# Cross attention's output and its sums regrouped through a scratch in DRAM instead of by TensorE transposes, with the queries in another order

## The chip, the core and the metric

The kernel runs on one core of a Trainium2 chip, in one launch. The core has five engines that take their instructions in order and work at the same time: TensorE (PE; its weight loads are listed apart as PEld), VectorE (DVE), ScalarE (ACT), GpSimd (POOL) and SyncE (SP), which here does nothing but issue DMAs. Matrix products land in PSUM, and this kernel cuts PSUM into eight banks. The metric is device time in microseconds (us), median of several runs. The kernel before takes 1217.6 us (three runs, 1217.3 to 1218.85).

## The reference

One layer of a perceiver in float32, for 4 sequences of 256 rows of 256 numbers, each with its own context of 4096 rows. Three parts are added to x one after the other: cross attention, a causal linear attention, and a gated feed-forward network. The change concerns the first.

```python
# B = 4 sequences, T = 256 queries, S = 4096 keys, D = 256, 16 heads of 16
Q = layernorm(x) @ Wq.T + bq
K = ctx @ Wk.T + bk
V = ctx @ Wv.T + bv
Q, K, V = (z.reshape(B, -1, 16, 16).transpose(0, 2, 1, 3) for z in (Q, K, V))
dot = einsum('bhsd,bhtd->bhst', Q, K) / sqrt(16)
out = einsum('bhst,bhtd->bhsd', softmax(dot), V)
out = out.reshape(B, T, D)          # the heads are not moved back
x = x + out @ Wh.T + bh
x = x + causal_linear_attention(layernorm(x))
x = x + feed_forward(layernorm(x))
```

The reshape at the end is what the change turns on. `out` has head, query and dimension as its axes, and it is read as 256 rows of 256 without a transpose. So row h*16 + s//16 of the matrix that Wh multiplies holds the 16 queries s = 16*(s//16) .. +15 of one head h, 16 dimensions each: query s stands in the 16 columns from 16*(s%16) on. The product with Wh sums over these columns, so TensorE needs them on partitions: a partition is a pair of s%16 and dimension, and eight values of s%16 make one half (one of the two k chunks) of 128 partitions.

## The kernel before

**Units and windows.** Cross attention is cut into 16 units u = 4b + q, one for each sequence b and group q of four heads. A unit goes through its 4096 keys in 16 windows of 256, so the main loop (L977) makes 256 windows n and one more. A head has 32 partitions: 16 dimensions, and beside them ones that yield the sum of the weights.

**One window.** In order of TensorE: the scores of the window, transposed (pt, L769, 16 matmuls of 256 columns), with the maxima products of a later unit between them (pm, L732, 8 matmuls of 512 columns); then half an item of a key or value product of a later pair of units (pk or pv, both issued by the helper `product4` at L159, 16 matmuls of 256 or 32 of 128 columns); then the product of the weights of the window before with its values (pav, L789, 16 matmuls). VectorE takes four maxima off pm (mx, L739) and adds pav to the unit's running sum (av: L797 in a unit's first window, L799 after). ScalarE makes the exponentials (e, L774) and takes pk and pv out of PSUM (ku, L675; v, L703). Every one of pt, pm, pk, pv, pav takes one of the eight PSUM banks in turn, and so waits for whoever reads the one that held it before. There are key and value items in the windows below n = 232, after which the start of the causal attention fills in; the maxima run out at n = 238.

**What a unit leaves.** av has 128 partitions, 32 for each of four heads, and 256 columns, the queries. In a head's 32 rows, rows 0 to 15 are the weighted sums by dimension and row 16 the sum of the weights, the denominator. A unit's last av is added in window 0 of the next unit, and there `finish(u - 1)` (L801, called at L1010) gives up to three pieces, which `later` (L1012) puts into windows 2, 8 and 10 of the running unit:

- `normalise` (L809): two TensorE transposes of av into pt_x (L815), so that queries are on partitions; a reciprocal of the eight denominators of each partition (rd, L819), a product (on, L821), the value bias added on POOL (L826), and eight DMAs from SP's queue (L830) that gather 16-number runs of on into the rows of xo, of which two units (q even, q odd) share one tile.
- `turn` (L835), for odd q only: two transposes of xo into px (L839) and VectorE's copy to oT (L840).
- `project` (L843), for odd q only: oT times Wh (py1, L847), added to the residual xr on VectorE (L848).

**The end.** Unit 15 has no unit after it. Its three pieces are returned (L1016) and placed by hand: `normalise()` at L541, before the first two loads of the feed-forward weights (`weight_load`, the w_i tiles, on SP's queue through L400) and the first steps of the causal attention; `turn15` and `project15` in the lists `fills[2]` and `fills[3]` (L549, L550). Each w_i is changed to float by ScalarE (`weight`, L405), and the list of fills has one of them in each of the steps 1 to 6. A step of the causal attention has products pa, masks on VectorE (at, L444) and products po (L453), and the feed-forward work follows in later steps.

**The queries.** `queries(b)` (L852) makes one sequence's queries. Its `turn` (L860) transposes the normalised rows by the helper `transposed` (L161): two TensorE transposes into a bank "tr" and one ScalarE copy (L167) to zT, for each half of 128 queries; `project` (L866) multiplies zT by Wq. The column of zT is the query number, and this order is kept by qT, the scores, e and av.

**Bias and other constants.** `load_rest` (L79) is called once, when the first unit's maxima are done (L970). It issues eleven loads on SP's queue, the first of which lays the value bias bv on all 128 partitions (bv_sb, L83). The context's tiles (L651, four buffers) and the rows of keys (L678) are issued by SP too.

**Order.** In both stretches of `manual_schedule` (L539, L883) the order of PE, ACT, DVE and SP is that of the program; POOL is not among them, and its place is set by the scheduler from what its instructions wait for. POOL's own DMA queue holds only the 16 small loads of bk_sb (L74) at the start.

Of the kernel before, what the change touches and what calls it, by code (L numbers as in the profile page):

```python
# [39 lines left out]
def perceiver_layer(  # L40
# [141 lines left out]
    lnp = ctx.enter_context(tc.tile_pool(name="lnp", bufs=2))  # L182
    psum = ctx.enter_context(tc.tile_pool(name="psum", bufs=8, space=PSUM))
# [107 lines left out]
    def start_causal():  # L291
# [78 lines left out]
        tc, xr, load_x, load_rest, ctxT, wq_sb, bq_sb, wkP, bk_sb, wvP, eps, ident, layernorm, transposed, product4,  # L370
        qT, kts, lnp, bank, rest, start_causal)
# [167 lines left out]
    with tc.manual_schedule(engines={ET.PE, ET.Activation, ET.DVE, ET.SP}):  # L539
        normalise, turn15, project15 = finish  # L540
        normalise()  # L541
# [7 lines left out]
        fills[2] += [turn15]  # L549
# [47 lines left out]
def cross_attention(tc, xr, load_x, load_rest, ctxT, wq_sb, bq_sb, wkP, bk_sb, wvP, eps,  # L597
                    ident, layernorm, transposed, product4, qT, kts, lnp, bank, rest, start_causal):
# [21 lines left out]
    with ExitStack() as st:  # L620
# [180 lines left out]
        def finish(u):  # L801

            b, q = divmod(u, NQ)
            av = avs.pop(u)

            def normalise():  # L809
                if q % 2 == 0:  # L810
                    rows_of[b] = lnp.tile([P, D], F32, tag="xo", name="xo")
                xo = rows_of[b]
                pt = bank([P, 2, 4, 32], "pt_x")
                for i in range(2):
                    nc.tensor.transpose(  # L815
                        pt[:, i].rearrange("p j r -> p (j r)"), av[:, i * P : (i + 1) * P], ident
                    )
                rd = lnp.tile([P, 2, 4], F32, tag="rd", name="rd")
                nc.vector.reciprocal(rd, pt[:, :, :, HD])  # L819
                on = lnp.tile([P, 2, 4, HD], F32, tag="on", name="on")  # L820
                nc.vector.tensor_tensor(  # L821
                    on, pt[:, :, :, :HD], rd.unsqueeze(3).to_broadcast([P, 2, 4, HD]), ALU.mult
                )
                bias = rest[0][:, 4 * q * (HD + 1) : 4 * (q + 1) * (HD + 1)].rearrange("p (h e) -> p h e", e=HD + 1)
                for i in range(2):
                    nc.gpsimd.tensor_tensor(on[:, i], on[:, i], bias[:, :, :HD], ALU.add)  # L826
                for i in range(2):
                    for j in range(4):
                        r0 = 64 * (q % 2) + 16 * j + 8 * i
                        nc.sync.dma_start(  # L830
                            out=xo[r0 : r0 + 8, :].rearrange("a (r d) -> a r d", d=HD),
                            in_=on[:, i, j, :],
                        )

            def turn():  # L835
                oT = lnp.tile([P, KC, P], F32, tag="oT1", name="oT1")
                px = bank([P, KC, P], "px")
                for k in range(KC):
                    nc.tensor.transpose(px[:, k, :], rows_of[b][:, k * P : (k + 1) * P], ident)  # L839
                nc.vector.tensor_copy(oT, px)  # L840
                rows_of[b] = oT

            def project():  # L843
                t, oT = 2 * b + q // 2, rows_of.pop(b)
                py = bank([P, D], "py1")
                for k in range(KC):
                    product4(py, oT[:, k, :], rest[1][:, k, :], start=k == 0, stop=k == KC - 1)  # L847
# [35 lines left out]
        with tc.manual_schedule(engines={ET.PE, ET.Activation, ET.DVE, ET.SP}):  # L883
# [93 lines left out]
            for n in range(NU * NS + 1):  # L977
# [113 lines left out]
```

## Time and profile before

| | us |
|---|---|
| runs of the kernel before | 1217.3, 1217.6, 1218.85 |
| the profiled execution | 1217.58 |
| its span, first to last instruction | 1215.9 |

So 1.7 us of the profiled execution lie outside its span. It stands within 0.1 us of the median of the runs, and sums made against it hold for the median.

The stages, with the time in which each engine was busy (TensorE's clock was granted in full, 0.99 to 1.00, in all of them):

| stage | us | PE | DVE | ACT | POOL | DMA share |
|---|---|---|---|---|---|---|
| first keys, queries, first maxima | 0 to 68 | 58.4 | 52.9 | 25.8 | 13.6 | 0.54 |
| loop: constants still loading | 68 to 152 | 82.4 | 64.6 | 50.5 | 6.1 | 0.37 |
| loop with key or value items | 152 to 900 | 747.3 | 575.5 | 456.7 | 6.9 | 0.30 |
| loop, through the start of the causal attention | 900 to 1018 | 118.0 | 97.0 | 67.6 | 9.1 | 0.14 |
| last unit without maxima | 1018 to 1068 | 47.5 | 32.6 | 36.4 | 10.8 | 0.02 |
| causal attention and feed-forward | 1068 to 1216 | 133.6 | 89.1 | 49.8 | 26.2 | 0.08 |

How to read the lines that follow. A group of instructions is named by its engine, its line in the program, its operation and the tiles that it writes and reads ("out<-in", each with partitions x elements). The number before a bar is how many there are; after it stand the total busy time and the mean in ns, and then the engine's idle time just before these instructions with what ended it. In a timeline each line is a run of equal instructions: start, length, engine and line, the count, and in brackets idle time just before it with the instruction that ended it. "SPq" and "POOLq" are DMAs issued from that engine's queue. In a table of stretches, after the stretch and its length, come the busy times of PE, PEld, DVE, ACT and POOL, then the granted clock, the share of the 16 DMA engines and the GB/s moved.

### The profile page before, as it was taken

The page shows a single profiled execution, that of the slowest core. Times are in us where ns is not written, and L with a number is a line of the kernel's source. Part 1 is how long each engine was busy: PE and PEld are TensorE (multiplying, and loading weights), DVE is VectorE, ACT ScalarE, POOL GpSimd, SP SyncE. Part 2 cuts the span into 40 slices and gives each one's busy share as a digit, 9 for nine tenths or more (in the row PEclk, how much of TensorE's full clock was granted, in tenths as well). Part 3 has the DMA queues.
Part 4 walks back from the last instruction along what each step waited for, and adds up shares of the span by engine and source line. Part 5 has one row for each costly group of instructions (what it writes and reads, how often), then busy time and mean ns, then how long its engine had stood idle before and what let it go on. Part 6 is the DMA issues. An engine that isn't in the chain of part 4 may idle for free.

```text
span 1215.9 us, 42635 instructions
## 1 busy us (share of the span) xinstructions
PE 1187.2 (98%) x18000; PEld 801.0 (66%) x18000; DVE 911.6 (75%) x1767; ACT 686.8 (56%) x1429; POOL 72.7 (6%) x147
## 2 busy tenths in 40 slices
PE   7999999999999999999999999999999999979998
PEld 3566667666766677667766776677667755546777
DVE  6887777777777777777777777777788887577653
ACT  3456666666566655665566655666566646853421
POOL 4010000000000000000000000000000102131210
PEclk9999999999999999999999999999999999999999
DMA  6452332233223421332223322322233000020000
GB/s 210 132 197 65 105 107 64 69 101 117 71 63 103 108 86 57 94 102 89 74 84 102 99 74 80 91 97 74 78 99 108 22 2 4 2 69 14 10 10 18
DMA packets 58190, 95.82 MB, mean 79 GB/s; under 512 B 29072, under 2 KB 31760, under 8 KB 58000
## 3 DMA queue, kind: packets, MB, share of 16 engines
q1 hardware_dynamic: 57072, 92.44, 25.3%
q8 instruction: 142, 2.33, 0.8%
q10 hardware_dynamic: 416, 0.66, 0.2%
q14 instruction: 48, 0.39, 0.1%
q0 software_dynamic: 512, 0.00, 0.0%
HBM read 74.17 MB, written 1.05 MB: 62 GB/s over the span
## 4 chain that ended last, share of the span: by engine, by line
PE 93%; DVE 5%; ACT 1%; DMA 1%; issue 0%; DVEq 0%; ACTq 0%
PE pt L769 22%; PE pm L732 18%; PE pav L789 18%; PE pv L159 11%; PE pk L159 11%; PE pd L530 2%; PE pg L518 2%; PE pu L518 1%; PE pq L870 1%; PE pqk L159 1%; PE pa L427 1%; PE py L492 1%; DVE kt L287 1%; DVE mx L739 1%; PE py L159 1%; PE po L453 1%
## 5 line engine op out<-in xcount | busy, mean ns | idle before, releaser
L774 ACT ACTIVATE e<-pt 128x512 f32<-128x512 f32 x1024 | 529.2, 602 | 381.2 <-PE pm L732 357.6
L739 DVE TENSOR_REDUCE mx<-pm 128x1 f32<-128x512 f32 x1024 | 635.6, 684 | 144.8 <-PE pm L732 144.8
L769 PE MATMUL pt<-qa,kt 32*128 32x256 f32 x4096 | 500.0, 388 | 1.3 <-DVE av L799 0.7
L732 PE MATMUL pm<-kt,qT 32*128 32x512 f32 x2048 | 494.6, 616 | 0.0
L769 PEld LDWEIGHTS pt<-qa,kt 32*128 32x128 f32 x4096 | 316.7, 184 | 117.8 <-ACT v L703 43.2
L789 PE MATMUL pav<-e,v 128*32 128x256 f32 x4096 | 269.6, 379 | 0.0
L732 PEld LDWEIGHTS pm<-kt,qT 32*128 32x128 f32 x2048 | 172.0, 184 | 15.6 <-issue 3.7
L789 PEld LDWEIGHTS pav<-e,v 128*32 128x32 f32 x4096 | 129.6, 110 | 72.5 <-issue 3.9
L799 DVE TENSOR_TENSOR av<-pav,av 128x256 f32<-128x256 f32 x240 | 101.8, 424 | 65.3 <-PE pav L789 65.1
L159 PE MATMUL pv<-wv_sb,ctx 128*32 128x128 f32 x4096 | 137.5, 276 | 0.0
L159 PE MATMUL pk<-ctx,wk_sb 128*32 128x256 f32 x2048 | 136.7, 388 | 0.0
L159 PEld LDWEIGHTS pv<-wv_sb,ctx 128*32 128x32 f32 x4096 | 104.2, 109 | 43.5 <-DVE mx L739 42.7
L159 PEld LDWEIGHTS pk<-ctx,wk_sb 128*32 128x32 f32 x2048 | 54.8, 110 | 67.1 <-DVE mx L739 39.0
L675 ACT ACTIVATE ku<-pk,bk_sb 128x256 f32<-128x256 f32 x128 | 63.2, 495 | 10.9 <-PE pk L159 9.6
L826 POOL TENSOR_TENSOR on<-on,bv_sb 128x64 f32<-128x64 f32 x32 | 9.2, 307 | 819.1 <-DVE on L821 819.1
L703 ACT COPY v<-pv 128x256 f32<-128x256 f32 x128 | 51.5, 402 | 9.9 <-PE pv L159 9.9
L288 ACT ACTIVATE kt<-kt,shift 128x512 f32<-128x512 f32 x32 | 22.4, 725 | 12.5 <-DVE kt L287 12.5
L444 DVE TENSOR_TENSOR at<-pa,mask 128x384 f32<-128x384 f32 x32 | 16.3, 551 | 14.2 <-PE pa L432 14.1
L287 DVE TENSOR_SCALAR kt<-pf,low,top 128x512 f32<-128x512 f32 x32 | 23.7, 804 | 2.8 <-PE pf L281 2.6
L518 PE MATMUL pg<-zT,wg 128*128 128x256 f32 x96 | 23.3, 386 | 0.7 <-ACT zT L510 0.7
L518 PE MATMUL pu<-zT,wu 128*128 128x256 f32 x96 | 22.7, 379 | 0.0
L530 PE MATMUL pd<-wd,hT 128*128 128x256 f32 x96 | 21.6, 381 | 0.0
(128 smaller groups left out, 563.4 us busy)
## 6 DMA issues: line engine op xcount, KB each, us to landing
ctx<-in_ctxT_dram SPq DMA_DIRECT2D x128, 512.0 KB
kt<-ku SPq DMA_DIRECT2D x508, 32.0 KB
xo<-on SPq DMA_DIRECT2D x128, 8.0 KB
xr<-in_x_dram SPq DMA_DIRECT2D x4, 256.0 KB
out_dram<-o SPq DMA_DIRECT2D x8, 128.0 KB
wqkv_sb<-in_wqkv_dram SPq DMA_DIRECT2D x1, 768.0 KB
w_i<-in_w_gate_dram SPq DMA_DIRECT2D x2, 384.0 KB
w_i<-in_w_up_dram SPq DMA_DIRECT2D x2, 384.0 KB
```

The source lines that it names most:

```text
L159: nc.tensor.matmul(out[js], lhsT=lhsT[:, js], rhs=rhs, **flags)
L287: nc.vector.tensor_scalar(f, pf.rearrange("p s t -> p (s t)"), low, top, ALU.max, ALU.min)
L518: nc.tensor.matmul(ps[:, i, :], lhsT=w[:, k, ns], rhs=zT[:, k, :], start=k == 0, stop=k == KC - 1)
L530: nc.tensor.matmul(pd, lhsT=hT[:, n, i * P : (i + 1) * P], rhs=wd[:, n, :], start=n == 0, stop=n == NH - 1)
L675: nc.scalar.activation(ku[:, cs], made.pop(), AF.Identity, bias=bk_sb[:, m : m + 1])
L703: nc.scalar.copy(to.rearrange("p t (h d) -> p t h d", d=HD + 1)[:, :, :, :HD], made.pop().rearrange("p t (h d) -> p t h d", d=HD),)
L732: nc.tensor.matmul(pm, lhsT=qT[rows, q, t0 : t0 + P], rhs=kt[rows, c * CH : (c + 1) * CH], start=True, stop=True,)
L739: nc.vector.tensor_reduce(mx[:, i, j, c : c + 1], pm, AX.X, ALU.max)
L769: nc.tensor.matmul(pt[:, i, :], lhsT=kt[rows, ks], rhs=qa[rows, :], start=True, stop=True)
L774: nc.scalar.activation(e, pt, AF.Exp, scale=0.25)
L789: nc.tensor.matmul(pav[32 * h : 32 * h + 32, :], lhsT=v[:, t % KT, c0 : c0 + 32], rhs=es[n, h][:, i, :], start=i == 0, stop=i == 1,)
L799: nc.vector.tensor_tensor(avs[u], pav, avs[u], ALU.add)
```

## The change

The transposes of a unit's result go. What they did (put queries on partitions, regroup into rows, put columns back on partitions) is done by DMAs through a scratch tile in DRAM, and av never passes TensorE again.

- **Queries in another order.** The ScalarE copy out of the bank "tr" now permutes: query s goes to column 16*(s%16) + s//16 of zT, where it went to column s. qT, the scores, e and av keep this order, so that the 16 columns of av with one remainder s%16, which belong to 16 different rows of the matrix that Wh multiplies, lie side by side. `transposed` is folded into `turn`, which has the same two transposes and one copy for each half as before; the copy's output is now strided.
- **Out to DRAM.** `finish(u)` at once issues four DMAs, one for each head, that write 17 rows of av (16 dimensions and the denominators) with their 256 columns to scr, in runs of 16 numbers (64 bytes).
- **Back.** For each half k, one DMA reads the sums into oT, whose partitions are the pairs of s%16 and dimension, and whose columns are 64 of the 128 rows (4 heads by 16 values of s//16) that two units share; and one reads the denominators into dn, each repeated over the 16 partitions that need it.
- **Queue.** These four writes and four reads a unit are issued by POOL for units 0 to 13 and by SP for units 14 and 15. The eight xo DMAs of a unit on SP are gone.
- **Divide.** `divide` is a reciprocal of dn in place (128 partitions x 128 numbers), a product into oT on VectorE, and the bias on POOL: two adds of 64 numbers a partition as before, now with a bias that depends on partition (dimension) and head. `project` is as before but reads this oT. The pieces `normalise` and `turn` are gone, and the two that are left go to windows 4 and 8.
- **Bias.** bvT replaces bv_sb: [128 partitions, 16 heads], made by eight DMAs on SP of 16 rows of 16 single numbers.
- **End.** Unit 15's DMAs are issued where `finish(15)` is called, in the loop's last pass; its divide is in `fills[2]`, where `turn15` was, and its project stays in `fills[3]`. The line `normalise()` goes.

```diff
+    bvT = const.tile([P, H], F32, tag="bvT", name="bvT")
+
     def load_rest():
 
         q = nc.sync
+        for r in range(P // HD):
+            q.dma_start(
+                out=bvT[r * HD : (r + 1) * HD, :],
+                in_=bvP[: H * (HD + 1)].rearrange("(h e) -> e h", e=HD + 1)[:HD],
+            )
         return (
-            load(bvP.partition_broadcast(P), [P, VW], "bv_sb", queue=q),
+            bvT,
             load(whT, [P, KC, D], "wh_sb", queue=q),
...
-    def transposed(dst, src):
-
-        n = src.shape[1] // P
-        ps = bank([P, n, P], "tr")
-        for k in range(n):
-            nc.tensor.transpose(ps[:, k, :], src[:, k * P : (k + 1) * P], ident)
-        nc.scalar.copy(dst, ps)
...
+    dram = ctx.enter_context(tc.tile_pool(name="dram", bufs=2, space=bass.MemoryType.DRAM))
...
-        normalise, turn15, project15 = finish
-        normalise()
+        divide15, project15 = finish
         for n in range(2):
             weight_load(n)
...
-        fills[2] += [turn15]
+        fills[2] += [divide15]
         fills[3] += [project15, norm3]
...
             b, q = divmod(u, NQ)
             av = avs.pop(u)
-
-            def normalise():
-                if q % 2 == 0:
-                    rows_of[b] = lnp.tile([P, D], F32, tag="xo", name="xo")
-                xo = rows_of[b]
-                pt = bank([P, 2, 4, 32], "pt_x")
-                for i in range(2):
-                    nc.tensor.transpose(
-                        pt[:, i].rearrange("p j r -> p (j r)"), av[:, i * P : (i + 1) * P], ident
-                    )
-                rd = lnp.tile([P, 2, 4], F32, tag="rd", name="rd")
-                nc.vector.reciprocal(rd, pt[:, :, :, HD])
-                on = lnp.tile([P, 2, 4, HD], F32, tag="on", name="on")
-                nc.vector.tensor_tensor(
-                    on, pt[:, :, :, :HD], rd.unsqueeze(3).to_broadcast([P, 2, 4, HD]), ALU.mult
+            queue = nc.sync if u >= NU - 2 else nc.gpsimd
+
+            scr = dram.tile([KC, T // 16 // KC, HD + 1, 4, 16], F32, tag="scr", name="scr")
+            for j in range(4):
+                queue.dma_start(
+                    out=scr[:, :, :, j].rearrange("k r e a -> e (k r) a"), in_=av[32 * j : 32 * j + HD + 1, :]
                 )
-                bias = rest[0][:, 4 * q * (HD + 1) : 4 * (q + 1) * (HD + 1)].rearrange("p (h e) -> p h e", e=HD + 1)
-                for i in range(2):
-                    nc.gpsimd.tensor_tensor(on[:, i], on[:, i], bias[:, :, :HD], ALU.add)
-                for i in range(2):
-                    for j in range(4):
-                        r0 = 64 * (q % 2) + 16 * j + 8 * i
-                        nc.sync.dma_start(
-                            out=xo[r0 : r0 + 8, :].rearrange("a (r d) -> a r d", d=HD),
-                            in_=on[:, i, j, :],
-                        )
-
-            def turn():
-                oT = lnp.tile([P, KC, P], F32, tag="oT1", name="oT1")
-                px = bank([P, KC, P], "px")
+            if q % 2 == 0:
+                rows_of[b] = lnp.tile([P, KC, 2, 4, 16], F32, tag="oT1", name="oT1")
+            oT = rows_of[b]
+            dn = lnp.tile([P, KC, 4, 16], F32, tag="dn", name="dn")
+            for k in range(KC):
+                queue.dma_start(out=oT[:, k, q % 2], in_=scr[k, :, :HD].rearrange("r e j a -> r e (j a)"))
+                queue.dma_start(
+                    out=dn[:, k],
+                    in_=scr[k, :, HD].rearrange("r j a -> r (j a)").unsqueeze(1).to_broadcast([P // HD, HD, 64]),
+                )
+
+            def divide():
+                nc.vector.reciprocal(dn, dn)
+                to = oT[:, :, q % 2]
+                nc.vector.tensor_tensor(to, to, dn, ALU.mult)
                 for k in range(KC):
-                    nc.tensor.transpose(px[:, k, :], rows_of[b][:, k * P : (k + 1) * P], ident)
-                nc.vector.tensor_copy(oT, px)
-                rows_of[b] = oT
+                    bias = rest[0][:, 4 * q : 4 * q + 4].unsqueeze(2).to_broadcast([P, 4, 16])
+                    nc.gpsimd.tensor_tensor(to[:, k], to[:, k], bias, ALU.add)
...
-            return [normalise] + ([turn, project] if q % 2 == 1 else [])
+            return [divide] + ([project] if q % 2 == 1 else [])
...
             def turn():
+
                 zT = lnp.tile([P, KC, T], F32, tag="zT1", name="zT1")
                 got.append(zT)
                 for i in range(2):
-                    transposed(zT[:, :, i * P : (i + 1) * P], z[:, i, :])
+                    ps = bank([P, KC, P], "tr")
+                    for k in range(KC):
+                        nc.tensor.transpose(ps[:, k, :], z[:, i, k * P : (k + 1) * P], ident)
+                    nc.scalar.copy(
+                        zT.rearrange("p k (r a) -> p k a r", a=16)[:, :, 8 * i : 8 * i + 8],
+                        ps.rearrange("p k (a r) -> p k a r", r=16),
+                    )
...
-                        for at, piece in zip((2, 8, 10), left):
+                        for at, piece in zip((4, 8), left):
                             later[n + at] = piece
```

More of the change, by code (lines that the diff above doesn't have):

```diff
@@ L369, in perceiver_layer @@
     finish = cross_attention(
-        tc, xr, load_x, load_rest, ctxT, wq_sb, bq_sb, wkP, bk_sb, wvP, eps, ident, layernorm, transposed, product4,
-        qT, kts, lnp, bank, rest, start_causal)
+        tc, xr, load_x, load_rest, ctxT, wq_sb, bq_sb, wkP, bk_sb, wvP, eps, ident, layernorm, product4,
+        qT, kts, lnp, dram, bank, rest, start_causal)
     wout_sb = rest[8]
@@ L597, in cross_attention @@
 def cross_attention(tc, xr, load_x, load_rest, ctxT, wq_sb, bq_sb, wkP, bk_sb, wvP, eps,
-                    ident, layernorm, transposed, product4, qT, kts, lnp, bank, rest, start_causal):
+                    ident, layernorm, product4, qT, kts, lnp, dram, bank, rest,
+                    start_causal):
     nc = tc.nc
@@ L838, in turn @@
                 for k in range(KC):
-                    nc.tensor.transpose(px[:, k, :], rows_of[b][:, k * P : (k + 1) * P], ident)
-                nc.vector.tensor_copy(oT, px)
-                rows_of[b] = oT
+                    bias = rest[0][:, 4 * q : 4 * q + 4].unsqueeze(2).to_broadcast([P, 4, 16])
+                    nc.gpsimd.tensor_tensor(to[:, k], to[:, k], bias, ALU.add)
             def project():
-                t, oT = 2 * b + q // 2, rows_of.pop(b)
+                t = 2 * b + q // 2
@@ L845, in project @@
+                del rows_of[b]
                 py = bank([P, D], "py1")
                 for k in range(KC):
-                    product4(py, oT[:, k, :], rest[1][:, k, :], start=k == 0, stop=k == KC - 1)
+                    product4(
+                        py, oT[:, k].rearrange("p q j a -> p (q j a)"), rest[1][:, k, :], start=k == 0, stop=k == KC - 1
+                    )
                 nc.vector.tensor_tensor(xr[:, t, :], py, xr[:, t, :], ALU.add)
-            return [normalise] + ([turn, project] if q % 2 == 1 else [])
+            return [divide] + ([project] if q % 2 == 1 else [])
@@ L863, in turn @@
                 for i in range(2):
-                    transposed(zT[:, :, i * P : (i + 1) * P], z[:, i, :])
+                    ps = bank([P, KC, P], "tr")
[4 more added lines that the diff above has]
+                        ps.rearrange("p k (a r) -> p k a r", r=16),
+                    )
             def project(q):
```

## The prediction

> **What bounds the kernel now.** I read the page's busy shares and its chain first, then the timeline of two attention windows, the groups by form, the waits and the end. A "window" below is one pass of the main loop (256 keys of one head group).
>
> ```profile
> PE 1187.2 (98%) x18000; PEld 801.0 (66%) x18000; DVE 911.6 (75%) x1767; ACT 686.8 (56%) x1429; POOL 72.7 (6%) x147
> PE 93%; DVE 5%; ACT 1%; DMA 1%; issue 0%; DVEq 0%; ACTq 0%
> ```
>
> TensorE is busy 98% and is 93% of the chain, so every TensorE instruction removed shortens the run, unless TensorE is then made to wait. Whether it waits is read in a window:
>
> ```profile
> 142.59 0.42 DVE L797 COPY av<-pav 128x256 f32<-128x256 f32 x1 [0.28 <-PE pav L789]
> 143.62 2.48 DVE L739 TENSOR_REDUCE mx<-pm 128x1 f32<-128x512 f32 x4 [0.61 <-PE pm L732]
> 144.38 0.59 PEld L159 LDWEIGHTS pk<-ctx,wk_sb 128*32 128x32 f32 x16 [0.33 <-DVE mx L739]
> 144.39 1.07 PE L159 MATMUL pk<-ctx,wk_sb 128*32 128x256 f32 x16
> 146.25 0.44 PE L815 MATMUL pt_x<-ident,av 128*128 128x128 f32 x2
> 146.39 0.42 DVE L799 TENSOR_TENSOR av<-pav,av 128x256 f32<-128x256 f32 x1 [0.28 <-PE pav L789]
> 146.73 0.20 DVE L819 RECIPROCAL rd<-pt_x 128x8 f32<-128x8 f32 x1
> 146.97 0.29 DVE L821 TENSOR_TENSOR on<-pt_x,rd 128x128 f32<-128x128 f32 x1
> ```
>
> The reader is to see that VectorE has a single hole of 0.61 us, between av and the first maximum (mx), and that the next product (pk, elsewhere pv) starts 0.08 us after that first maximum ends (143.62 + 0.68 = 144.30): it takes the PSUM bank that this maximum frees. So 75% busy is not slack: whatever VectorE does beyond the hole delays TensorE one for one, and no later wait gives it back.
>
> **What is removed.** From one av to the next is 3.80 us in a plain window. In the windows that hold the two pt_x transposes it is 4.17 for two units and 4.27 for the twelve after; with the two px transposes it is 4.17. So units 0 to 13 give 2 x 0.37 + 12 x 0.47 = 6.3 us, and seven px pairs give 7 x 0.37 = 2.6: **-8.9 us**. The 4.27 is itself the mechanism above: there "on" starts 0.26 us after rd, a PSUM bank comes free late, and 0.10 us is lost.
>
> **What is added on VectorE.** The divide now works with dimensions on partitions: a reciprocal of 128 numbers a partition where it was 8, then a 128-wide product. The trace has no such reciprocal; three rows bound it:
>
> ```profile
> L819 DVE RECIPROCAL rd<-pt_x 128x8 f32<-128x8 f32 x16 | 3.3, 205 | 0.5 <-PE pt_x L815 0.5
> L471 DVE RECIPROCAL den<-den 128x16 f32<-128x16 f32 x8 | 2.0, 253 | 0.3
> L112 DVE RECIPROCAL ln_rs<-ln_rs 128x2 f32<-128x2 f32 x4 | 0.6, 160 | 4.1 <-ACT ln_rs L109 4.1
> ```
>
> From 2 to 16 elements, both in SBUF, it grows by 93 ns, 6.64 ns an element: 160 + 126 x 6.64 = 1.00 us. The flattest pair (8 to 16) gives 0.93. The Trainium skill ("VectorE: DVE Perf Modes", section "First, the fixed hardware budget") says that reciprocal is an iterated divide with a repeat count of 8; with that page's 0.96 GHz it is 8.33 ns an element, 1.21 us. I take the rows' 1.00. In order after av: 0.34 to the reciprocal's start (146.39 to 146.73), 1.00, a gap of 0.26 (the product waits for two landings and the reciprocal, like the twelve late "on"), and 0.23 until the next instruction starts (0.29, overlapped by 0.06 as the four maxima are). The first maximum comes 1.83 us after av instead of 1.03: 0.80 late, 0.05 of it covered. The program places the divide in windows with pk or pv for 14 units: 14 x 0.75 = **+10.5 us** (5 with 0.93 and a gap of 0.04; 13.5 by the rule). The loop alone nets +1.6.
>
> The bias adds go to POOL, as before (307 ns each, 6% busy). ScalarE's eight zT copies (0.37 each) write with a stride; one pair stands on the path, at 8.62 us: between 0 and +0.7, taken as 0. The load of bvT is eight issues of 16-row, single-element runs in place of one of 0.42: 3 to 5 us more on SP at 69 us, with 1.6 idle there and then four buffers of context ahead (77.77 to 95.97 is waiting): 0.
>
> **The trip through DRAM, units 0 to 13.** POOL issues four writes, waits for them, then issues four reads. The divide stands four windows later, 4 x 3.80 = 15.2 us of cover. The only rows of POOL's queue are the bk_sb loads: 0.48 us an issue, 2.7/5.1/6.7 us (min/median/max) to landing in a stretch where the DMA engines are 93% busy. With 2.7: 0.1 + 4 x 0.48 + 2.2 + 3.0 of data (next paragraph) + 4 x 0.48 + 2.2 = 11.4 us, hidden; with 5.1 it is 16.2, with 6.7 19.4. A write has 272 runs where bk_sb has 16; SP's issue hardly grows with runs (kt, 16 runs: 0.59; xo, 128 runs: 0.61), so I keep 0.48, and the loop's DMA share is 0.2 to 0.4, so I take **hidden, 0**. If it is late, each microsecond costs 14, because DVE waits in order with the maxima behind it.
>
> **How many engines a write uses.** Packets:
>
> ```profile
> 1070.00:1072.00 2.00, 2.00 (x28) 1.53 (x30) 2.00 (x4) 1.17 (x2) 0.34 (x1) 1.00 0.14 13
> DMA packets 58190, 95.82 MB, mean 79 GB/s; under 512 B 29072, under 2 KB 31760, under 8 KB 58000
> ```
>
> In the first row (a window with only xo's 64-byte runs) a share of 0.14 of 16 engines over 2 us moves 26 kB, 406 packets: 11 ns each. A write here (17 rows x 16 runs of 64 bytes) spread like xo costs nothing. But the Trainium skill ("DMA: Bandwidth & Descriptors", section "Why a DMA increments its semaphore by 16 and not by 1") says that a DMA uses the largest number of engines up to 16 that divides the slowest dimension of both sides; 17 leaves one, on SP's queue the same one each time. The page agrees where it can: 29072 small packets, less 16384 of xo, 128 of bq_sb, 512 single words and 11024 completions of the other 689 DMAs, leave 1024 for xo's 128 DMAs, eight each, as 128 and 8 rows give. By spreading a unit's four writes take 0.7 us of data, by the rule 4 x 272 x 11 = 12.0 on SP's queue (3.0 on POOL's, if each write takes another engine). I take the rule, at 11 ns; a write to DRAM may cost more than the SBUF row: 20 ns would add 10.
>
> **Units 14 and 15 are on SP.** Chain: 0.6 + 12.0 + 1.7 (w_i's latency, 2.7 less its data) + 4 x 0.61 + 2.1 = 18.8 us. Unit 14's av ends at 1018.0 and the divide is due behind the av of 1034.6: 2.2 late. VectorE is the busy one there, and its own work grows by 1.0: **+3.2**. The end:
>
> ```profile
> 1066.47 0.42 DVE L799 TENSOR_TENSOR av<-pav,av 128x256 f32<-128x256 f32 x1 [1.79 <-PE pav L789]
> 1068.54 5.28 SPq L830 DMA_DIRECT2D xo<-on  x8
> 1073.93 0.85 SPq L400 DMA_DIRECT2D w_i<-in_w_gate_dram  x2
> 1077.10 0.84 ACT L405 ACTIVATE wg<-w_i 128x768 f32<-128x768 int32 x1 [2.36 <-DMA w_i<-in_w_gate_dram]
> 1082.67 0.41 DVE L840 COPY oT<-px 128x256 f32<-128x256 f32 x1
> 1083.01 1.01 DVE L444 TENSOR_TENSOR at<-pa,mask 128x384 f32<-128x384 f32 x2
> ```
>
> Gone are TensorE's 0.9 (pt_x and its wait) and ScalarE's 2.36: in the built program the first w_i load now stands before the scratch writes. So VectorE reaches the divide at 1079.5. The data lands at 1067.0 + 18.8 = 1085.8; with 1.00 + 0.26 + 0.29 the masks (L444) start at 1087.3, not 1083.0: **+4.3**. Behind the divide stand the masks, on which TensorE's po waits; POOL's bias stands before its own masks. With the writes spread it is -2.5.
>
> **Sum**, against the profiled execution (1217.58, span 1215.9; the median of the runs is 1217.6): -8.9 + 10.5 + 3.2 + 4.3 = +9.1, **1226.7 us**.
>
> **Rivals.** (1) The 17-row writes spread over the engines. Then units 14 and 15 are hidden: -8.9 + 10.5 + 0.6 - 2.5 = -0.3, **1217.3**, not slower; with the cheap end of the divide 1212. For it: 11 ns packets and idle engines. Against: the count above. It decides when a unit's four writes take under about 6 us. (2) POOL's trip is late: 18 us instead of under 15.2 gives 14 x 2.8 = 39, **1266**; at 16.2 it is 1241. For it: the median landing of 5.1 and the unseen issue price; against: that stretch's 93% DMA load. It decides above 15.2.
>
> **How the numbers follow.** Forecast 0.45 (1219 to 1241: divide 5 to 13.5, packets 11 to 20 ns), rival 1 0.28, rival 2 0.27. Within 0.2% (2.4 us, about what a measurement of this kernel can tell from no change): 0.15, mostly rival 1. Faster 0.16, slower 0.69. The range 1213 to 1260 leaves out rival 1's cheapest divides and rival 2 beyond about 2.5 us late.
>
> **What would show it.** Windows with a divide near 4.55 us from av to av and the reciprocal near 1.00 us; no DVE idle time before it on a DMA in units 0 to 13, but some in 14 and 15; scratch writes at 1 completion each; no ScalarE wait for w_i. A reciprocal under 0.5 us, or the DVE waiting in every unit, would make the prediction wrong.

## The result and the profile after

The changed kernel takes **1424.8 us** (four runs, 1424.2 to 1427.5), the kernel before 1217.5 beside it: a ratio of **1.170** (95% interval 1.169 to 1.172). Forecast was 1226.7, with a range to 1260. The profiled execution is 1424.22 us, its span 1422.5.

The busy shares, the chain and two groups of the page, in the order of the page:

```profile
PE 1208.4 (85%) x17952; PEld 810.8 (57%) x17952; DVE 922.5 (65%) x1759; ACT 690.0 (49%) x1429; POOL 212.1 (15%) x259
...
PEclk9999898998989898989899998989898989998999
...
PE 63%; DMA 15%; POOL 7%; DVE 6%; issue 6%; ACT 1%; SPq 1%; POOLq 0%; DVEq 0%; ACTq 0%
...
L815 POOL DMA_DIRECT2D scr<-av x56 | 107.6, 1926 | 688.8 <-DVE av L800 625.5
...
L830 DVE RECIPROCAL dn<-dn 128x128 f32<-128x128 f32 x16 | 15.2, 953 | 180.4 <-DMA dn<-scr 180.4
```

TensorE has 48 instructions fewer and is still busy for 21 us more, because once in every unit its clock is granted only in part (the row PEclk, in tenths; it had nines alone before). A fifth of the chain is now DMA and POOL. VectorE sits idle for 180.4 us before the reciprocal, until the denominators (dn) land. The new reciprocal itself takes 953 ns, near the 1.00 us that was forecast.

One unit in the timeline. Unit 0's last sum ends at 140.03; its divide stands four windows later:

```profile
139.60 0.43 DVE L800 TENSOR_TENSOR av<-pav,av 128x256 f32<-128x256 f32 x1 [0.28 <-PE pav L790]
140.32 5.80 POOL L815 DMA_DIRECT2D scr<-av  x3 [55.36 <-DVE av L800]
...
150.11 1.92 POOL L815 DMA_DIRECT2D scr<-av  x1 [3.99 <-issue]
...
154.79 0.42 DVE L800 TENSOR_TENSOR av<-pav,av 128x256 f32<-128x256 f32 x1 [0.28 <-PE pav L790]
...
164.32 0.61 POOL L823 DMA_DIRECT2D oT<-scr  x1 [12.29 <-DMA scr<-av]
...
169.24 0.95 DVE L830 RECIPROCAL dn<-dn 128x128 f32<-128x128 f32 x1 [14.03 <-DMA dn<-scr]
...
171.18 1.93 PE L167 MATMUL pk<-ctx,wk_sb 128*32 128x256 f32 x16 [14.52 <-DVE mx L740]
172.88 1.93 PE L790 MATMUL pav<-e,v 128*32 128x256 f32 x16
...
176.69 1.07 PE L167 MATMUL pk<-ctx,wk_sb 128*32 128x256 f32 x16
```

From the end of av (140.03) to the reciprocal (169.24) are 29.2 us, of which 15.2 were covered. An issue of a write takes POOL 1.92 us; the fourth is held up by 3.99 more, for which the trace names no cause; the last write lands 12.29 after the end of its issue; the four reads and their landing take 4.9. VectorE, which could have divided at 155.2, waits 14.03 us with the four maxima behind it, and TensorE's pk, which needs the bank that the first maximum frees, waits 14.52. And then pk and pav, 16 matmuls each, take 1.93 us, where pk takes 1.07 a window later. The granted clock (the column before the DMA share, after the busy times of PE, PEld, DVE, ACT and POOL) says why:

```profile
158.00:169.00 11.00, 0.00 (x0) 0.00 (x0) 0.00 (x0) 0.03 (x1) 2.38 (x4) 0.64 0.55 138
169.00:171.00 2.00, 0.00 (x0) 0.00 (x0) 1.73 (x3) 0.00 (x0) 0.40 (x2) 0.50 0.00 0
171.00:173.00 2.00, 1.82 (x20) 0.91 (x24) 1.92 (x4) 0.00 (x0) 0.14 (x1) 0.50 0.00 0
...
175.00:177.00 2.00, 2.00 (x32) 1.43 (x32) 1.38 (x3) 0.65 (x2) 0.00 (x0) 1.00 0.27 61
```

While TensorE idles its clock falls to one half, and it comes back to full only after 3.6 us of work at half rate.

The account of the 206.6 us between the two spans: units 1 to 14, each with the divide of the unit before it, are longer by 11.5 to 17.1 us, 200.5 together. In their fourteen gaps TensorE is idle for 180.3 us; the half-rate work behind them sums to 56.4 us, of which half, 28.2, is lost; the removed transposes give back 8.9. That makes 199.6 of the 200.5. The rest of the 206.6 is 0.8 before the first sum and 5.4 from unit 15 to the end.

### The profile page after: what moved, and what is told of

Read it like the earlier page. It is cut to its first block, busy times and chain, and to the rows that moved or that the text cites. A ratio compares the mean times of both kernels' runs of the same rounds, so it can differ in the third digit from the quotient of the medians.

```text
span 1422.5 us, 42525 instructions
## 1 busy us (share of the span) xinstructions
PE 1208.4 (85%) x17952; PEld 810.8 (57%) x17952; DVE 922.5 (65%) x1759; ACT 690.0 (49%) x1429; POOL 212.1 (15%) x259
## 4 chain that ended last, share of the span: by engine, by line
PE 63%; DMA 15%; POOL 7%; DVE 6%; issue 6%; ACT 1%; SPq 1%; POOLq 0%; DVEq 0%; ACTq 0%
PE pt L770 14%; PE pav L790 13%; DMA scr<-av 12%; PE pm L733 11%; PE pv L167 8%; PE pk L167 8%; POOL scr L815 6%; DMA dn<-scr 3%; PE pd L531 1%; PE pg L519 1%; DVE mx L740 1%; PE pu L519 1%; PE pq L874 1%; POOL oT L823 1%; DVE dn L830 1%
## 5 line engine op out<-in xcount | busy, mean ns | idle before, releaser
L770 PEld LDWEIGHTS pt<-qa,kt 32*128 32x128 f32 x4096 | 320.6, 186 | 128.6 <-ACT v L704 43.2
L790 PE MATMUL pav<-e,v 128*32 128x256 f32 x4096 | 281.1, 392 | 0.3 <-DVE av L800 0.3
L167 PE MATMUL pk<-ctx,wk_sb 128*32 128x256 f32 x2048 | 142.4, 401 | 103.7 <-DVE mx L740 103.7
L815 POOL DMA_DIRECT2D scr<-av x56 | 107.6, 1926 | 688.8 <-DVE av L800 625.5
L167 PE MATMUL pv<-wv_sb,ctx 128*32 128x128 f32 x4096 | 143.5, 284 | 76.6 <-DVE mx L740 76.6
L167 PEld LDWEIGHTS pv<-wv_sb,ctx 128*32 128x32 f32 x4096 | 108.2, 113 | 121.5 <-DVE mx L740 120.0
L830 DVE RECIPROCAL dn<-dn 128x128 f32<-128x128 f32 x16 | 15.2, 953 | 180.4 <-DMA dn<-scr 180.4
L823 POOL DMA_DIRECT2D oT<-scr x28 | 16.8, 601 | 148.6 <-DMA scr<-av 148.6
L288 DVE TENSOR_SCALAR kt<-pf,low,top 128x512 f32<-128x512 f32 x32 | 23.7, 804 | 2.3 <-PE pf L282 2.3
```

The source lines that it names most:

```text
L167: nc.tensor.matmul(out[js], lhsT=lhsT[:, js], rhs=rhs, **flags)
L770: nc.tensor.matmul(pt[:, i, :], lhsT=kt[rows, ks], rhs=qa[rows, :], start=True, stop=True)
L790: nc.tensor.matmul(pav[32 * h : 32 * h + 32, :], lhsT=v[:, t % KT, c0 : c0 + 32], rhs=es[n, h][:, i, :], start=i == 0, stop=i == 1,)
L815: queue.dma_start(out=scr[:, :, :, j].rearrange("k r e a -> e (k r) a"), in_=av[32 * j : 32 * j + HD + 1, :])
L823: queue.dma_start(out=oT[:, k, q % 2], in_=scr[k, :, :HD].rearrange("r e j a -> r e (j a)"))
```

## The experiments

**First question: is it only that the trip is late?** The two first runs move the divide and the project to later windows and leave all else.

```diff
-                        for at, piece in zip((4, 8), left):
+                        for at, piece in zip((10, 12), left):   # late10
+                        for at, piece in zip((6, 10), left):    # late6
```

> Divide and project stand 10 and 12 windows after a unit's last sum instead of 4 and 8; everything else as changed. Theory A (the trip through POOL's queue is simply too long: 29.0 us in the trace against a cover of 4 x 3.80 = 15.2): with 38 us of cover all fourteen stalls go, and with them the half-rate stretch of TensorE behind each. What is left is +0.8 for the strided query copies, -8.9 for the transposes, 14 x about 0.48 = +6.7 for a divide with the measured 0.95 us reciprocal and its 0.04 us gap, and about +5.4 for units 14 and 15: 1217.6 + 4.0 = 1221.6, in 1218 to 1226. Theory B (the scratch traffic hurts beside the wait, by keeping the DMA engines 86% busy while keys and context tiles want them): more than 1240, with TensorE waiting outside the windows that hold a divide.

Measured: **1225.1 us**, ratio 1.0065 (1.0048 to 1.0081). So the lateness of the divide is nearly all of it: 199.7 of the 207.3 us are gone with 38 us of cover. Unit 0's divide now starts without a wait:

```profile
178.20 0.94 DVE L830 RECIPROCAL dn<-dn 128x128 f32<-128x128 f32 x1
```

The writes are as slow as before (1.92 us an issue, median landing 12.0) and the DMA engines as busy (shares of 0.86 to 0.96 in each stretch of 4 us from 144 to 160). SP feels it: its eight issues of key rows beside them take 12.5 us, where they take 5.4 behind sp16's writes. But TensorE loses little by it in the loop. Two places are longer for no reason of the divide's or the project's. One is a window of unit 4, by 1.1 us; what it waits for the trace doesn't say. The other is the passage from unit 13 to unit 14, by some 1.3 us: an instruction of VectorE there (z, L328) takes 1.40 us beside POOL's issue of a write, where it takes 0.41 elsewhere. The same z takes as long in the changed kernel and in late6, and in no run with cheaper issues. So the traffic does cost something beside the wait, but 2 us and not the 20 of theory B. Of the 7.6 us by which its span is longer than that of the kernel before, 7.1 stand after the last sum, where unit 15 still goes out through SP in 17 rows.

> Divide and project stand 6 and 10 windows after a unit's last sum; everything else as changed. VectorE waited 12.5 us a unit at 4 windows, so at 6 it should wait 12.5 - 7.6 = 4.9 us. Theory A1 (each late microsecond costs one, and TensorE's half clock after a long idle time costs 1.9 more a unit only if the idle time is long): the clock stays full after a 5 us stall: 1221.6 + 14 x 4.9 = 1290. Theory A2 (every stall is followed by the half-rate stretch): 14 x 1.9 = 27 more, 1317.

Measured: **1331.5 us**, ratio 1.093 (1.091 to 1.095). VectorE waits 83.0 us for dn in the fourteen units, 5.9 each, where 4.9 was expected; A2's 1317 with 14 x 1.0 more is 1331. TensorE has thirteen gaps of 4.8 to 10.4 us here, and every one is followed by 2.9 to 4.7 us of work at half rate (47.3 together, so 23.7 lost where 27 was expected). One gap of 5.3 us, from 236.83 to 242.13, and the work behind it, with the granted clock as above:

```profile
239.20:242.10 2.90, 0.00 (x0) 0.00 (x0) 1.87 (x4) 0.00 (x0) 0.54 (x2) 0.51 0.05 11
242.10:246.00 3.90, 3.87 (x52) 2.46 (x56) 1.93 (x4) 0.37 (x1) 0.00 (x1) 0.50 0.17 29
```

So a stall of 5 us pays nearly the same clock as one of 14. A2 holds.

**Second question: the queue, or the shape of the write?** sp17 gives all units to SP; sp16 does too, and writes 16 rows a head, with the four denominators in a write of their own.

```diff
-            queue = nc.sync if u >= NU - 2 else nc.gpsimd
+            queue = nc.sync
...
-                    out=scr[:, :, :, j].rearrange("k r e a -> e (k r) a"), in_=av[32 * j : 32 * j + HD + 1, :]
+                    out=scr[:, :, :HD, j].rearrange("k r e a -> e (k r) a"), in_=av[32 * j : 32 * j + HD, :]
                 )
+            queue.dma_start(
+                out=scr[:, :, HD].rearrange("k r j a -> j (k r) a"),
+                in_=av.rearrange("(j r) s -> j r s", r=32)[:, HD],
+            )
```

> All sixteen units' scratch DMAs are issued by SP, divide at 4 windows as in the change. Unit 14 on SP took 18.6 us from the end of its sum to the divide, so units 0 to 13 should be about 3.0 us late each, too short for the clock to fall: 1221.6 + 14 x 3.0 = 1264. Rival (SP is held by the writes, 3.1 us an issue, so that key rows and context tiles behind them on the same queue come late): more than 1290, with TensorE or ScalarE waiting on a DMA outside the divide's window.

Measured: **1317.1 us**, ratio 1.081 (1.079 to 1.082). More than the 1264, but not by the rival's mechanism: outside the divide's window and the one behind it no window of the loop is longer for it. Two terms were too small. VectorE waits 6.4 to 7.3 us in every other unit, beginning with the first, and 2.8 to 3.3 in those between, 68.8 over the fourteen where 42 was expected; and eleven of TensorE's fourteen gaps are followed by half-rate work, 50.6 us of it, of which 25.3 are lost. 1264 + 26.8 + 25.3 is 1316.

> As sp17, but each head's write has 16 rows (the dimensions), and the four denominators of a unit go in a fifth write of 4 rows. Theory C (a write of 17 rows uses one DMA engine on SP's queue, one of 16 rows uses sixteen): the data takes about 1.2 us instead of 4 x 272 x 18 ns = 19.6 us on one engine, the issues fall to about 0.6 us, the trip to 9 to 11 us, and the divide is never waited for in units 0 to 13: 1216 to 1224, and the end gets shorter too. Theory D (the number of 64-byte runs sets it, whatever engines they go to): the trip stays near 18.6 us and the time stays within 10 us of sp17.

Measured: **1217.5 us**, ratio 0.9994 (0.9985 to 1.0003). One row taken out of each write is worth 100 us on this queue. The timelines of unit 0, first sp17, then sp16:

```profile
141.75 10.66 SPq L815 DMA_DIRECT2D scr<-av  x4
...
157.92 0.70 SPq L823 DMA_DIRECT2D oT<-scr  x1
...
161.97 0.95 DVE L830 RECIPROCAL dn<-dn 128x128 f32<-128x128 f32 x1 [6.63 <-DMA dn<-scr]
```

```profile
143.05 1.86 SPq L815 DMA_DIRECT2D scr<-av  x4
...
144.96 0.67 SPq L818 DMA_DIRECT2D scr<-av  x1
...
148.50 0.65 SPq L827 DMA_DIRECT2D oT<-scr  x1
...
156.17 0.42 DVE L800 TENSOR_TENSOR av<-pav,av 128x256 f32<-128x256 f32 x1 [0.28 <-PE pav L790]
156.51 0.94 DVE L834 RECIPROCAL dn<-dn 128x128 f32<-128x128 f32 x1
...
157.49 0.29 DVE L836 TENSOR_TENSOR oT<-oT,dn 128x128 f32<-128x128 f32 x1
157.70 2.48 DVE L740 TENSOR_REDUCE mx<-pm 128x1 f32<-128x512 f32 x4
```

The first read is issued 16.2 us after the first write with 17 rows, and 5.5 after it with 16, for the same bytes in runs of the same 64 bytes. In sp16 the divide has no wait in brackets: the last read's issue ended 5.4 us before it.

**Third question: rows or runs?** Two more shapes on SP's queue, one with as many runs cut otherwise, one with nearly twice the runs.

```diff
# sp98: as sp17, but (lines that only move to the right are not marked)
+                for e0, e1 in ((0, 9), (9, HD + 1)):
                     queue.dma_start(
-                        out=scr[:, :, :, j].rearrange("k r e a -> e (k r) a"), in_=av[32 * j : 32 * j + HD + 1, :]
+                        out=scr[:, :, e0:e1, j].rearrange("k r e a -> e (k r) a"),
+                        in_=av[32 * j + e0 : 32 * j + e1, :],
# sp32: as sp17, but
-            scr = dram.tile([KC, T // 16 // KC, HD + 1, 4, 16], F32, tag="scr", name="scr")
+            scr = dram.tile([KC, T // 16 // KC, 32, 4, 16], F32, tag="scr", name="scr")
...
-                    out=scr[:, :, :, j].rearrange("k r e a -> e (k r) a"), in_=av[32 * j : 32 * j + HD + 1, :]
+                    out=scr[:, :, :, j].rearrange("k r e a -> e (k r) a"), in_=av[32 * j : 32 * j + 32, :]
```

> As sp17, with each head's 17 rows written as 9 rows and 8 rows: the same 272 runs and bytes a head, eight writes a unit. Theory C (a write goes to as many engines as the largest number up to 16 that divides its rows: 9 and 8 here, 1 for 17): the data takes 4 x 144 x 18 / 9 = 1.2 us and as much for the other half, the issues about 0.45 each, the trip 8 x 0.45 + 3 + 2.4 + 2.1 = 11 us, hidden: 1216 to 1221. Theory F (any number of rows that leaves a rest by 16 goes to one engine): the four writes of 9 rows take 4 x 144 x 18 ns = 10.4 us on one engine, the trip is 17 to 19 us and late by 1 to 3: 1235 to 1265.

> As sp17, with all 32 rows of a head written, 512 runs of 64 bytes where it were 272. Theory C (rows decide: 32 has 16 as a divisor): twice the data still takes only 4 x 512 x 18 / 16 = 2.3 us, the trip is about 10 us, hidden: 1216 to 1221. Theory D (runs decide): 512 runs would make the trip nearly twice as long as with 272, 30 us and more, with 14 stalls of 15 us: over 1430.

Measured: sp98 **1217.3 us** (ratio 0.9994, 0.9985 to 1.0003), sp32 **1217.6** (0.9994, 0.9986 to 1.0003). The reads are issued 6.3 and 5.8 us after the first write. Rows decide on this queue, not runs, and an odd number of rows is no harm as such (theories D and F fall). How many engines a write uses can be counted from the page. Its rows of packets, for sp17, sp16, sp98 and sp32 in this order:

```profile
DMA packets 68990, 97.84 MB, mean 74 GB/s; under 512 B 40000, under 2 KB 42560, under 8 KB 68800
```

```profile
DMA packets 70014, 97.84 MB, mean 80 GB/s; under 512 B 41024, under 2 KB 43584, under 8 KB 69824
```

```profile
DMA packets 70015, 97.85 MB, mean 80 GB/s; under 512 B 41024, under 2 KB 43584, under 8 KB 69824
```

```profile
DMA packets 85310, 98.83 MB, mean 81 GB/s; under 512 B 56320, under 2 KB 58880, under 8 KB 85120
```

The data is the same small packets in the first three, so the number under 512 B differs by completions alone, one of 4 bytes from each engine used. With 1 for each of the 64 writes of 17 rows, 16 for 16 rows and 4 for 4, sp16 should have 64 x 16 + 16 x 4 - 64 = 1024 more than sp17; it has 1024. With 9 and 8, sp98 should have 64 x (9 + 8) - 64 = 1024 more; it has. sp32 has 64 x 15 x 16 = 15360 runs and 64 x 15 = 960 completions more; it has 16320 more. The rule of the Trainium skill that the prediction weighed ("DMA: Bandwidth & Descriptors", section "Why a DMA increments its semaphore by 16 and not by 1") holds to the packet on SP's queue.

**Fourth question: is it the same on POOL's queue?** Three shapes, all else as in the change: pool16 has sp16's writes, pool98 sp98's, and pool_rows writes 17 rows, each in one run of 1 KB. In pool_rows the sums do not reach their places, the regrouping is left out.

```diff
# pool_rows
-                    out=scr[:, :, :, j].rearrange("k r e a -> e (k r) a"), in_=av[32 * j : 32 * j + HD + 1, :]
+                    out=scr.rearrange("k r e j a -> (k r e j a)").rearrange("(h e s) -> h e s", h=4, s=T)[j],
+                    in_=av[32 * j : 32 * j + HD + 1, :],
```

> As the change (POOL for units 0 to 13, divide at 4 windows), but each head's write has 16 rows, and the denominators go in a fifth write of 4 rows, for all units. Theory C (17 rows on one DMA engine is the cause on POOL's queue too, as it was on SP's): the trip falls from 29 us to under 15.2, the stalls go, 1214 to 1224. Theory E (POOL's queue has its own price for runs of 64 bytes: 1.92 us an issue of 272 runs, a 4 us gap before the fourth, some 12 us until the last one lands, with the DMA engines 86% busy at 26 GB/s): 256 runs cost nearly what 272 do, and a fifth issue comes on top: the trip stays between 26 and 31 us, 1395 to 1450.

> As the change, with 17 rows in each write, but each row of 256 sums goes to the scratch as one run of 1 KB where it went as 16 runs of 64 bytes. The reads are unchanged, so the sums reach other places of the output: the regrouping is left out. Theory E (it is the number of runs on POOL's queue): an issue takes about 0.5 us as with the bk_sb loads (16 runs, 0.48), data 1 to 2 us, and the trip 4 x 0.5 + 3 + 2.4 + 2.5 = 10 us, hidden: 1216 to 1226. Theory C (17 rows on one engine, whatever their runs): 4 x 17 KB on one engine at the 79 to 159 ns that 2 to 4 KB packets take in this trace is about 3 us, so it would be hidden by this theory as well; what tells them apart here is the issue: 1.9 us if the rows set it, 0.5 if the runs do.

> As the change (POOL for units 0 to 13), with each head's 17 rows written as 9 and 8. On POOL's queue 17 rows of 64-byte runs cost 1.92 us an issue and some 12 us of data, 16 rows 0.57 and 2, and 17 rows of one 1 KB run 0.53 and 2. Theory G (it is the cutting of a write that 17 rows spoil, 9 and 8 rows do not): 8 issues at about 0.5 us, then 2 + 2.4 + 2.5 = 11 us: 1216 to 1222. Theory H (on this queue only 16 rows are cut well): the trip stays above 25 us, over 1380.

Measured: pool16 **1217.9 us** (0.9998, 0.9989 to 1.0006), pool_rows **1217.1** (0.9997, 0.9989 to 1.0006), pool98 **1217.4** (0.9995, 0.9986 to 1.0003). The stalls are gone in all three. What an issue of a write costs POOL (ns, min/median/max), in the change, pool16, pool_rows and pool98:

```profile
L815 POOL DMA_DIRECT2D scr<-av x56: 1906/1920/1977, 140.3 to 1149.6; - x56
```

```profile
L815 POOL DMA_DIRECT2D scr<-av x56: 562/566/605, 141.3 to 952.7; - x56
```

```profile
L815 POOL DMA_DIRECT2D scr<-av x56: 505/525/551, 140.9 to 952.0; - x56
```

```profile
L816 POOL DMA_DIRECT2D scr<-av x112: 594/605/667, 140.6 to 954.4; - x112
```

So neither 17 rows alone (pool_rows has them) nor many runs of 64 bytes alone (pool16 has 256 a write, pool98 144 and 128) make a write dear on this queue; both together do. Theories E and H fall, and G fits. One rival to G is left: the dear write is also the only one on this queue with more than 256 runs (272), and no run here has more than 256 with another number of rows. On SP's queue sp32, with 512, rules that out; on POOL's it stays open.

What POOL's queue carries in the whole execution (packets, MB, share of the 16 DMA engines), in the change and in pool16:

```profile
q0 software_dynamic: 7680, 3.76, 11.7%
```

```profile
q0 software_dynamic: 4544, 2.86, 1.6%
```

In the trace's records of single packets, between 140 and 170 us, the change's POOL queue has 240 of 256 bytes (median 717 ns each) where pool16 has 68 of 1024 bytes (79 ns) for nearly the same data; pool98 has 68 of 1024 bytes too. The dear writes are thus cut into smaller pieces, each of which takes nine times as long. And it is not one engine that carries them, as on SP's queue: up to 16 of the 256-byte packets are under way at once, where of sp17's packets there are never more than three, and the DMA engines' share is 0.86 from 150 to 156 us. Why they are cut so, and why each takes so long, stays open.

**A version that beats both.** The hole on VectorE is 0.61 us, and the divide of 0.94 + 0.29 doesn't fit. Cut in three, each piece does. Split is sp16 with

```diff
...
-            def divide():
-                nc.vector.reciprocal(dn, dn)
+            def inverse(k):
+                return lambda: nc.vector.reciprocal(dn[:, k], dn[:, k])
+
+            def divide():
                 to = oT[:, :, q % 2]
...
-            return [divide] + ([project] if q % 2 == 1 else [])
+            return [inverse(0), inverse(1), divide] + ([project] if q % 2 == 1 else [])
...
-                        for at, piece in zip((4, 8), left):
+                        for at, piece in zip((4, 5, 6, 8), left):
```

> As sp16, with the divide in three pieces: the reciprocal of one half (64 numbers a partition) in window 4, of the other in window 5, the product in window 6; the project stays in window 8. A window has a hole of 0.61 us on VectorE between av and the first maximum. The reciprocal of 128 numbers took 0.95 us and one of 16 took 0.25, so one of 64 should take 0.55 and start 0.34 us after av: it ends before the first maximum's product is there, and so does the product of 0.29. Theory (the divide's +0.47 us a window is only what sticks out of the hole): 14 x 0.47 = 6.6 us less than sp16's 1217.5, 1210.9. Rival (a piece delays the first maximum whatever its length, by the gap and the fixed cost of one instruction more): 42 pieces at 0.1 to 0.2 us instead of 14 at 0.47, 1215 to 1219.

Measured: **1210.6 us**, ratio **0.9939** (0.9927 to 0.9952). Three windows of unit 1 in its timeline:

```profile
156.26 0.42 DVE L800 TENSOR_TENSOR av<-pav,av 128x256 f32<-128x256 f32 x1 [0.28 <-PE pav L790]
156.60 0.54 DVE L834 RECIPROCAL dn<-dn 128x64 f32<-128x64 f32 x1
157.29 2.48 DVE L740 TENSOR_REDUCE mx<-pm 128x1 f32<-128x512 f32 x4
...
160.06 0.42 DVE L800 TENSOR_TENSOR av<-pav,av 128x256 f32<-128x256 f32 x1 [0.28 <-PE pav L790]
160.40 0.54 DVE L834 RECIPROCAL dn<-dn 128x64 f32<-128x64 f32 x1
...
163.85 0.42 DVE L800 TENSOR_TENSOR av<-pav,av 128x256 f32<-128x256 f32 x1 [0.28 <-PE pav L790]
164.20 0.28 DVE L838 TENSOR_TENSOR oT<-oT,dn 128x128 f32<-128x128 f32 x1
```

From av to av it stays 3.80 us with a piece or without one, and the first maximum starts 1.03 us after av as it did before. This is the gain that the change was able to bring: the transposes' time, with VectorE's price hidden. From the first sum to the last the loop is 10.1 us shorter than in the kernel before (9.0 of it the transposes of units 0 to 13, the rest in units 13 and 15), and 6.8 remain between the spans, since the first sum comes 2.3 us later and the end is 1.1 longer.

## Why the prediction was wrong, step by step

- **The step that failed: "hidden, 0" for the trip of units 0 to 13.** The chain of 11.4 us had the right links, but wrong sizes, and one wait was missing. An issue was kept at bk_sb's 0.48 us because "SP's issue hardly grows with runs"; on POOL it is 1.92, 5.8 more for the four. A wait of 3.99 before the fourth issue had no term. Data and landing of the last write were given 3.0 + 2.2; they take 12.3. The reads' 4 x 0.48 + 2.2 measured 4.9. The whole is 29.2, where 15.2 were covered. With the median landing of its only rows the prediction had 16.2 itself, late already, and it took the shortest landing. Even its upper end, 19.4, fell short: it varied the landing of a 16-run DMA and left the issue price of a 272-run one at 0.48, though no row showed it.
- **The rival named the mechanism.** VectorE waits 172.9 us in the fourteen units, 12.3 each, which is what rival 2 described and what the prediction named as a sign that it is wrong. With that, the rival's own sum gives 1217.6 - 8.9 + 7.3 (the divide, below) + 172.9, and 28.2 for the clock, 0.8 before the first sum and 5.4 from unit 15 on: 1423.3, against 1424.2. Its size, 2.8 us late, was too small.
- **No term for the clock.** 28.2 us come from TensorE's half rate behind a gap. The Trainium skill has the rule ("TensorE: Matmul & The Clock Gate", section "Part 1: The HAM clock gate": half rate after one idle window of about 3.4 us, full rate again after about as long a busy one), and the rows of 158 to 177 us above agree with it: full clock after 3.6 us of work. Over all gaps (last section) the clock falls from 2.1 us on, sooner than the page's window, and comes back after up to 6.0 us. A rival that makes TensorE wait has to carry this term.
- **How many engines a write uses: right on SP's queue**, by 1024 completions. For unit 14 the prediction has 14.3 us from the first write to the first read, and the trace 14.1 (1219.31 to 1233.41); the packets of the four writes run for 12.0 us in sp17's unit 0, as forecast. What fell is the bracket "3.0 on POOL's, if each write takes another engine": unit 0's 256-byte packets run from 144.3 to 160.7, 16.4 us, though many are under way at once.
- **-8.9 for the transposes: right** (its terms, redone, add up to 9.0). In late10 the former pt_x windows are 0.37 (units 1, 2) and 0.45 to 0.47 shorter, the former px windows 0.33 to 0.37.
- **+10.5 for the divide: 7.3.** In sp16 a divide's window is 0.47 to 0.52 us longer, not 0.75 (0.91 and 0.57 in units 13 and 14). The reciprocal takes 0.94 (the line through the rows said 1.00, the estimate from the repeat count 1.21: the rows were nearer), and the gap before the product is 0.04 where 0.26 was taken from "on". The first maximum comes 1.53 us after av. The cheap end of the prediction, with 0.93 and a gap of 0.04, describes this case; its sum is 14 x 0.46 = 6.5, not the 5 that it states. That VectorE has no slack but this hole is shown from both sides, by sp16 and by split.
- **The queries' copies: taken as 0, at most 0.7.** They are on the path more often than at 8.62 us: a strided copy takes 608 ns where it took 375, and in sp16 the maxima fall behind by 0.37 at three later pairs, 1.1 us. The two groups, of before and of after:

```profile
L167 ACT COPY zT<-tr 128x256 f32<-128x256 f32 x8 | 2.7, 375 | 1.8 <-PE tr L166 1.7
```

```profile
L865 ACT COPY zT<-tr 128x256 f32<-128x256 f32 x8 | 4.1, 608 | 1.3 <-PE tr L864 1.2
```

- **Unit 14, +3.2: 0.2.** Its divide's window is 3.1 us longer, and the two windows behind it are 2.3 and 0.6 shorter than before. The step took VectorE for the bound there; it isn't.
- **The end, +4.3: 6.1.** The mechanism is the one forecast:

```profile
1267.11 0.37 SPq L401 DMA_DIRECT2D w_i<-in_w_gate_dram  x1
...
1267.52 10.36 SPq L815 DMA_DIRECT2D scr<-av  x4
...
1277.92 3.11 SPq L401 DMA_DIRECT2D w_i<-in_w_gate_dram  x1
...
1287.48 0.95 DVE L830 RECIPROCAL dn<-dn 128x128 f32<-128x128 f32 x1 [5.45 <-DMA dn<-scr]
...
1289.19 1.50 PE L167 MATMUL py<-wh_sb,oT 128*32 128x256 f32 x10 [7.40 <-POOL oT L835]
```

  From the end of av (1267.49) to the divide are 20.0 us, forecast 18.8. TensorE's gap of 7.4 us is followed by 5.2 us of work at half rate, against 3.1 behind the gap of 4.0 that stands in the kernel before. The w_i loads are no longer waited for at first, but later ones are held up by the writes (ScalarE waits 1.1 and 3.4 us). In sp16 the end costs 0.6.
- **Rival 1, 1217.3 if the writes spread over the engines:** sp16 and sp98 are that case, and measure 1217.5 and 1217.3. That they agree so closely is luck in part: in sp16 the divide costs 3.2 us less than the rival's sum has it, and the end 3.1 more (+0.6, not -2.5).

## What to carry to other kernels

Before a transpose is traded for a trip through DRAM, count the rows of each DMA: one with 17 rows runs on one engine of SP's queue. The same bytes as four writes of 16 rows and one of 4, or as 9 and 8 rows a head, were free of it, on POOL's queue too. Where work is put a fixed number of windows behind an unmeasured DMA chain, bound each link by its own shape (runs an issue, not only bytes), and put the work as late as the buffers allow: here six windows more would have hidden even the slow trip. A late VectorE step that keeps TensorE waiting costs more than its lateness, since every gap of over 4 us looked at here was followed by 2.7 to 6.0 us at half rate; and a step that doesn't fit into an engine's hole may fit in pieces.

## What the runs showed of the hardware that was not expected

- **A gap of over 4 us on TensorE always brought the half clock, and a longer gap did not cost more.** In the changed kernel, late6 and sp17, all 40 such gaps were followed by work at half rate, 2.7 to 6.0 us of it (half of that lost). Of the seven gaps between 3.3 and 3.8 us in sp17, four were. The clock falls 2.1 to 5.4 us after the gap begins, so a gap of 5 us loses nearly as much as one of 16.
- **A reciprocal on VectorE takes 6.0 to 6.3 ns more for each element of a partition**: 253 ns for 16, 541 for 64, 943 for 128, all at 128 partitions.
- **On POOL's queue a write of 17 rows of 64-byte runs costs 1.92 us an issue**, 3.4 times what 16 rows cost, and its packets of 256 bytes take 717 ns each (median), with up to 16 under way at once. Beside such an issue one instruction of VectorE took 1.40 us and not 0.41.
